# Causal attention in a two-layer hybrid model: queries and keys projected in the heads' own order, then moved to their fields

## The chip, the core and the metric

The kernel runs on one core of one Trainium2 chip. Its time is the device time of one execution in microseconds (us). A core has five engines with a queue of instructions each, which they work through in order: TensorE (PE; matrix products, with weight loads PEld listed apart), VectorE (DVE), ScalarE (ACT), GpSimd (POOL) and SyncE (SP, which issues DMAs). They wait for each other by semaphores. Matrix products read SBUF and write PSUM, which has eight banks of 128 partitions by 512 fp32 values.

## What is computed

A residual stream of 32 sequences of 256 tokens with 128 features passes through eight blocks. The change touches one of them, the last attention:

```python
x = x + _L1_attn_a_ref(_layernorm(x), ...)      # window attention with latents
x = x + _L1_ffn_ref(_layernorm(x), ...)         # 8 experts, 2 of them for each token
x = x + _L1_attn_b_ref(_layernorm(x), Wq, Wk, Wv, Wo)
x = x + _L1_ffn_ref(_layernorm(x), ...)

def _L1_attn_b_ref(x, Wq, Wk, Wv, Wo):          # 16 heads of 8 features
    Q, K, V = split(x @ Wq.T), split(x @ Wk.T), split(x @ Wv.T)
    Q, K = apply_rope(Q), apply_rope(K)         # turns pairs of neighbouring features
    scores = einsum(Q, K) / sqrt(8)             # causal, -inf for later keys
    out = softmax(scores) @ V
    return out @ Wo.T
```

## The kernel before

The stream is kept in SBUF, transposed, as 16 tiles `xs[c]` of 128 features by 512 tokens (a **chunk**: two sequences of 256). The stage `l1_attn_b` runs one generator, `chunk(c)`, for each of them; each `yield` ends a step. `pipeline(chunk, 16, newest=True)` (L336) starts a new chunk every 16 rounds and in each round takes one step of every active chunk, the newest first. A chunk has about 60 steps, so four chunks are in work at a time, 16 steps apart. What is written in this order is then put into queues by a scheduler, which may take a later instruction first where an earlier one is not ready; a tile waits for a free buffer of its tag.

The steps of a chunk, with their lines:

- Steps 0 to 8: `fetch` (L1420) reads the experts' rows of the block before and adds them to x (L1430 to L1434); `norm` (L323) centers (L326), squares, takes the mean (L311), the power -0.5 on GpSimd (L315) and spreads it (L320). L1634 gives `xin`, the normalised chunk.
- Steps 9 to 12, the part that changes: query and key are projected and turned. The 16 heads are laid out in two groups (y = 0, 1), 8 heads each with 16 partitions: 8 features and 8 spare ones, a **field**. The weights carry that layout already (`spaced`, L87), so that one 128x128 weight block makes one group. For each group and for q and k there are two products (L1643), one with the weights and one with the features of each pair swapped; VectorE multiplies them from PSUM with the cosine and the sine table (L1644); the two are added, for q by GpSimd (L1646), for k by VectorE (L1648), which also puts 1 into a spare feature of the field (the table `ninth`). `by_parity` (L940) then makes two masked copies of each key group on VectorE (L944).
- Steps 13 to 24: `attend` (L947) finds the largest score of each query: masks (L932), scores (L969, L996), reductions on VectorE (L978, L1000).
- Steps 25 to 28: the negated maximum is transposed (L1019) and added to the query's spare feature (L1021), masked copies `qb` (L944); the values are projected (L1149) and copied by VectorE (L1154).
- Steps 30 to 46: exponentials by key (L1038 and L1056 the scores, L1047 and L1060 the exponentials on ScalarE), GpSimd clears what is not causal (`keep_where`, L936), the weighted values (L1074), their copy on ScalarE (L1087), denominators (L1111) and their reciprocal `rden` (L1115), the result (L1119, L1120), the projection Wo (L1663).
- Steps 47 to 59: `send` (L1190) prepares the expert block: norm, router, shared expert, and eight indirect DMAs on GpSimd (L1301), which write the tokens into the experts' rows.

So the projections of a chunk (steps 9 to 12) stand in the same rounds as steps 25 to 28 of the chunk before, steps 41 to 44 of the one before that (L1074, L1087, L1111, L1115), and steps 57 to 58 of the third one before (L1301).

PSUM is handed out by tag: `st` has five banks for the scores, `av` one, and all else shares the tag `m` with two:

```python
ps = ph.enter_context(tc.tile_pool(name="cps", bufs=2, space=PSUM))
...
rps = ps.tile([P, CH], F32, tag="m", name="rps")
```

After the stage, `blocks1()` runs the experts on blocks of 256 rows (L1393, L1402); its first row loads wait for all of the rows that L1301 wrote.

Of the kernel before, what the change touches and what calls it, by code (L numbers as in the profile page):

```python
# [94 lines left out]
def pack_inputs(i):  # L95
    mam, com, att, row, taps = (Packed() for _ in range(5))
    turn = np.arange(DI).reshape(2, 32, 4).transpose(0, 2, 1).reshape(DI)

    p = "L0_attn_a_"
    for s in "fb":  # L100

        w = i[p + "in_w_" + s]
        mam.add("in_w" + s, np.concatenate([w[:DI], w[DI:][turn]]).T)


        xp = i[p + "xp_w_" + s]
        turned = [xp[at : at + DS].reshape(4, 4, DI).transpose(1, 0, 2).reshape(DS, DI) for at in (DTR, DTR + DS)]
        mam.add("xp" + s, halves(np.concatenate([xp[:DTR], *turned, np.zeros((1, DI), np.float32)]).T))
        mam.add("out" + s, i[p + "out_w_" + s][:, turn])
        dtp = np.zeros((DTR + 2 * DS + 1, DI), np.float32)  # L110
        dtp[:DTR], dtp[-1] = i[p + "dtp_w_" + s].T, i[p + "dtp_b_" + s]
        mam.add("dtp" + s, dtp)
        mam.add("conv_b" + s, i[p + "conv_b_" + s].reshape(1, -1))

        a = np.asarray(i[p + "A_log_" + s]).reshape(2, 32, 4, 4, 4)
        mam.add("A_log" + s, a.transpose(1, 4, 0, 3, 2).reshape(P, 32))
        mam.add("D" + s, halves(i[p + "D_" + s]))
        taps.add(s, i[p + "conv_w_" + s][:, 0, :].T.reshape(1, -1))
    mam.add("one_row", np.eye(DTR + 2 * DS + 1, dtype=np.float32)[:, -1:])
    mam.add("turn", np.eye(P, dtype=np.float32)[:, turn[:P]])  # L120
    mam.add("proj", halves(i[p + "proj_w"].T))
    mam.add("proj_b", col(i[p + "proj_b"]))
    mam.add("g", col(i[p + "ln_gamma"]))
    mam.add("minus", np.full((P, 1), -1.0))
    mam.add("b", col(i[p + "ln_beta"]))

    p = "L0_ffn_"
    com.add("pw", i[p + "pw_w"].T)
    com.add("dw", i[p + "dw_kernel"][:, 0, :])
    com.add("dw_b", col(i[p + "dw_bias"]))  # L130
    com.add("pw_b", col(i[p + "pw_b"]))
    com.add("rt0", i[p + "router_w"].T)
    com.add("exp_w", i[p + "expert_w"].transpose(2, 0, 1))
    com.add("exp_b", i[p + "expert_b"].T)
    com.add("f0_out", i[p + "out_w"].T)
    com.add("f0_out_b", col(i[p + "out_b"]))
    com.add("norm_w", col(i[p + "norm_w"]))
    com.add("ffd", i[p + "ff_down_w"].T)
    com.add("ffd_b", col(i[p + "ff_down_b"]))
    com.add("ffu", i[p + "ff_up_w"].T)  # L140
    com.add("ffu_b", col(i[p + "ff_up_b"]))
    row.add("rt0_b", i[p + "router_b"].reshape(1, -1))

    p = "L0_attn_b_"
    for n in "ABC":
        com.add("rnn" + n, i[p + n].T)
    com.add("rnn_g", col(i[p + "gamma"]))
    com.add("rnn_b", col(i[p + "beta"]))

    p = "L1_attn_a_"  # L150
    for n, part in (("q", 0), ("k", 1)):
        w = i[p + "qkv_w"][:, part * P : (part + 1) * P]
        b = i[p + "qkv_b"][part * P : (part + 1) * P].reshape(1, P)
        for x in range(2):
            att.add(f"a{n}{x}", spaced(w, x))
            att.add(f"ab{n}{x}", spaced(b, x).T)
    att.add("wv", i[p + "qkv_w"][:, 2 * P :])
    row.add("bv", i[p + "qkv_b"][2 * P :].reshape(1, -1))
    att.add("rq", i[p + "rq_w"])
    att.add("rq_b", col(i[p + "rq_b"]))  # L160
    att.add("rkv", i[p + "rkv_w"])
    att.add("rk_b", col(i[p + "rkv_b"][:32]))
    row.add("rv_b", i[p + "rkv_b"][32:].reshape(1, -1))
    att.add("rout", i[p + "rout_w"])
    att.add("rout_b", col(i[p + "rout_b"]))
    att.add("aout", i[p + "out_w"])
    att.add("aout_b", col(i[p + "out_b"]))
    for n in ("gl", "gr"):

        g = np.zeros((H, HD, H, HD), np.float32)  # L170
        for h in range(H):
            g[h, :, h, :] = i[p + n + "_w"]
        att.add(n, g.reshape(P, P))

    p = "L1_attn_b_"
    swap = np.arange(P) ^ 1
    for n in ("Wq", "Wk"):
        for x in range(2):
            att.add(f"{n}{x}", spaced(i[p + n].T, x))
            att.add(f"{n}s{x}", spaced(i[p + n][swap].T, x))  # L180
    att.add("Wv", i[p + "Wv"].T)
    att.add("Wo", i[p + "Wo"].T)

    p = "L1_ffn_"
    att.add("f1_g", col(i[p + "ln_gamma"]))
    att.add("f1_b", col(i[p + "ln_beta"]))
    att.add("rt1", i[p + "router_w"])
    att.add("sgu", i[p + "shared_gate_up_w"])
    att.add("sdn", i[p + "shared_down_w"])
    gu = np.ascontiguousarray(i[p + "gate_up_w"])  # L190
    dn = np.ascontiguousarray(i[p + "down_w"].reshape(E, FF // P, P, P).transpose(0, 2, 1, 3))

    return mam, com, att, row, taps, gu, dn


def shape_constants():
# [14 lines left out]
    for x in range(2):  # L211
        pk, dn = np.zeros((2, 8, 16, H, HD), np.float32)
        for h in range(8):
            pk[h, :HD, 8 * x + h, :] = np.eye(HD)
            dn[h, HD, 8 * x + h, :] = 1.0
        c1.add(f"pack{x}", pk.reshape(P, P))
        c1.add(f"den{x}", dn.reshape(P, P))
    c1.add("earlier", (np.arange(P)[:, None] < np.arange(P)[None]).astype(np.float32))
    c1.add("ones", np.ones((P, P), np.float32))
# [19 lines left out]
    inv = np.float32(10000.0) ** (-np.arange(half, dtype=np.float32) * np.float32(2.0) / np.float32(HD))  # L239
    ang = (np.arange(L, dtype=np.float32)[:, None] * inv[None]).astype(np.float32)  # L240
    at = (feat % HD) // 2
    used = (feat % 16 < HD)[:, None]
    cos = np.cos(ang)[:, at].T * used
    sin = np.sin(ang)[:, at].T * np.where(feat % 2 == 0, -1.0, 1.0)[:, None] * used
    c1.add("cosq", cos * SCALE)
    c1.add("sinq", sin * SCALE)
    c1.add("cosk", cos)
# [27 lines left out]
def hybrid_kernel(ctx: ExitStack, tc, x_d, out_d, d, packs):  # L275
# [1345 lines left out]
    def l1_attn_b(fetch, send):  # L1621
        with ExitStack() as ph:
            p1 = ph.enter_context(tc.tile_pool(name="c1", bufs=1))
            p2 = ph.enter_context(tc.tile_pool(name="c2", bufs=2))
            p3 = ph.enter_context(tc.tile_pool(name="c3", bufs=2))
            ps = ph.enter_context(tc.tile_pool(name="cps", bufs=2, space=PSUM))
            buffers = attention_buffers(p1)

            def chunk(c):
                x = xs[c]  # L1630
                yield from fetch(c, p2, ps, 4)
                xin = p2.tile([P, CH], F32, tag="xin", name="xin", bufs=2)
                xc, rb = yield from norm(p2, ps, x, 1)
                nc.vector.tensor_mul(xin, xc, rb)  # L1634
                yield
                rot, kb = {}, []
                for y in range(2):
                    for n in "qk":
                        t = p2.tile([P, CH], F32, tag=f"rot{n}{y}", name=f"rot{n}{y}", bufs=2 if n == "q" else 3)
                        u = p2.tile([P, CH], F32, tag="rot2", name="u")  # L1640
                        for w, tab, dst in ((f"W{n}{y}", "cos" + n, t), (f"W{n}s{y}", "sin" + n, u)):
                            rps = ps.tile([P, CH], F32, tag="m", name="rps")
                            nc.tensor.matmul(rps, W(w), xin, start=True, stop=True)  # L1643
                            nc.vector.tensor_mul(two(dst), two(rps), K(tab).unsqueeze(1).to_broadcast([P, 2, L]))  # L1644
                        if n == "q":
                            nc.gpsimd.tensor_add(t, t, u)  # L1646
                        else:
                            nc.vector.scalar_tensor_tensor(t, u, K("ninth"), t, ALU.add, ALU.add)  # L1648
                            kb.append(by_parity(p2, t, f"kb{y}", 1))
                        rot[n, y] = t  # L1650
                        yield
                o = p2.tile([P, CH], F32, tag="o", name="o")
                vbs, nms = buffers(c)

                def values(b):
                    project_values(ps, xin[:, b * L : (b + 1) * L], W("Wv"), None, vbs[b])
                    return vbs[b]

                yield from attend(
                    (p2, p3, ps), *([rot[n, y] for y in range(2)] for n in "qk"), kb, values, nms, masks_b, o  # L1660
                )
                ops = ps.tile([P, CH], F32, tag="m", name="ops")
                nc.tensor.matmul(ops, W("Wo"), o, start=True, stop=True)  # L1663
                nc.vector.tensor_add(x, x, ops)
                yield
                yield from send(c, p2, ps)

            pipeline(chunk, 16, newest=True)
# [47 lines left out]
```

## Time and profile before

| | us |
|---|---|
| median of 3 runs (6236.38 to 6243.42) | 6238.78 |
| the profiled execution | 6234.39 |
| its span, first to last instruction | 6232.7 |
| busy in the span: PE, PEld | 5356.8 (86%), 2792.6 (45%) |
| busy: DVE, ACT, POOL | 4117.2 (66%), 2710.2 (43%), 3289.4 (53%) |
| mean granted TensorE clock | 0.902 of full |

All numbers on lines and waits are of the profiled execution. A busy share is an average over stages with different limits: the recurrences of the first layer take the first half of the span, the window attention runs from about 3120 to 4150 us, the first expert pass to 4690, the stage of the change to about 5775, the second expert pass to the end.

The instructions that the change touches, over the whole stage: L1643 256 records (128 products of 128x512, each in two records), L1644 128 of 0.69 us, L1646 32 of 1.27 us, L1648 32 of 0.74 us at the median (1.04 in the mean), L944 on the keys 64 of 0.48 us.

In the answers of the trace a line gives the start and length in us, the engine, the line of the kernel, the operation with the tiles written and read, and in brackets the idle time of the engine before it with the instruction that ended it. Matrix products overlap, and their ends are modelled.

### The profile page before, as it was taken

How to read it: one execution, taken by the hardware profiler on the slowest of the kernel's cores; microseconds unless marked ns; L12 is line 12 of the kernel's file. 1: busy time of each engine (PE TensorE's matmuls, PEld its weight loads, DVE VectorE, ACT ScalarE, POOL GpSimd, SP SyncE). 2: the span in 40 equal slices, each digit the busy share in tenths (PEclk: the TensorE clock that was granted, in tenths of full speed). 3: DMA queues.
4: the chain of work that ended last, by engine and by line, in shares of the span. 5: the costliest groups of instructions: out<-in, count | busy, mean ns of one | idle time of the engine just before them, and what ended most of it. 6: DMA issues, size and time to landing. Idle time of an engine off the chain costs nothing. (4 is left out here: it accounts for less than half of the span.)

```text
span 6232.7 us, 73938 instructions
## 1 busy us (share of the span) xinstructions
PE 5356.8 (86%) x25850; PEld 2792.6 (45%) x25922; DVE 4117.2 (66%) x7006; ACT 2710.2 (43%) x4424; POOL 3289.4 (53%) x3074
## 2 busy tenths in 40 slices
PE   6777777777777799999998888897998999997997
PEld 2222222222221466965544444445884444443886
DVE  5998999989989554044555555655665666665565
ACT  4665666666655354344434444342221333333221
POOL 5888888888888564044634444443332333333332
PEclk9888988888988899598989999998998999998998
DMA  3333333333332740000000000004550000000555
GB/s 148 123 123 116 123 116 123 116 123 116 126 112 109 304 185 1 1 1 1 1 1 10 9 8 8 11 8 129 186 172 19 20 16 18 18 11 12 188 188 189
DMA packets 190421, 512.13 MB, mean 82 GB/s; under 512 B 22177, under 2 KB 75169, under 8 KB 164961
## 3 DMA queue, kind: packets, MB, share of 16 engines
q1 hardware_dynamic: 172192, 468.00, 21.1%
q0 software_dynamic: 17280, 35.69, 1.7%
q8 instruction: 205, 3.36, 0.2%
q10 hardware_dynamic: 576, 3.71, 0.2%
q14 instruction: 168, 1.37, 0.1%
HBM read 359.93 MB, written 147.38 MB: 81 GB/s over the span
## 5 line engine op out<-in xcount | busy, mean ns | idle before, releaser
L612 POOL TENSOR_TENSOR dBu<-widedu,bcB 128x512 f32<-128x512 f32 x1024 | 1294.8, 1284 | 249.9 <-DVE h L621 162.0
L621 DVE TENSOR_TENSOR_SCAN h<-dA,dBu 128x512 f32<-128x512 f32 x768 | 942.5, 1227 | 119.8 <-ACT dA L608 30.4
L574 PE MATMUL yps<-pr,cst_t 128*32 128x512 f32 x2048 | 579.9, 645 | 244.8 <-POOL pr L569 102.7
L936 POOL TENSOR_SCALAR_AFFINE_SELECT e<-e 128x2048 f32<-128x2048 f32 (+1 forms) x256 | 343.3, 1353 | 597.2 <-ACT e L1047 386.1
L1412 POOL DMA_INDIRECT rows_out<-y,goes x284 | 271.8, 957 | 559.9 <-DVE y L1410 464.2
L1000 DVE TENSOR_REDUCE nm<-st 128x2 f32<-128x512 f32 x512 | 324.3, 684 | 268.5 <-PE st L996 267.4
L608 ACT ACTIVATE dA<-widedelta,Af 128x510 f32<-128x510 f32 x512 | 348.5, 688 | 300.9 <-DVE h L621 222.0
L608 ACT ACTIVATE dA<-widedelta,Ab 128x510 f32<-128x510 f32 x512 | 345.0, 686 | 272.7 <-DVE h L621 209.5
L1187 ACT ACTIVATE s<-s 128x512 f32<-128x512 f32 x284 | 179.0, 630 | 578.3 <-DVE s L1186 309.2
L574 PEld LDWEIGHTS yps<-pr,cst_t 128*32 128x32 f32 x2048 | 86.8, 112 | 704.8 <-POOL pr L569 228.0
L315 POOL TENSOR_TENSOR rstd<-var,cst_t 128x4 f32<-128x4 f32 x128 | 130.0, 1016 | 516.2 <-DVE var L313 514.4
L781 POOL TENSOR_TENSOR comb<-comb,ye 128x512 f32<-128x512 f32 x224 | 284.8, 1275 | 182.0 <-DVE ye L780 75.2
L1060 ACT ACTIVATE e<-st 128x512 f32<-128x512 f32 x512 | 272.0, 598 | 184.5 <-PE st L1056 154.8
L569 POOL TENSOR_TENSOR pr<-hs,bcC 128x512 f32<-128x512 f32 x256 | 334.4, 1306 | 13.7 <-DVE hs L621 13.7
L621 DVE TENSOR_TENSOR_SCAN hs<-dA,dBu 128x512 f32<-128x512 f32 x256 | 308.3, 1204 | 48.8 <-ACT dA L608 47.3
L1301 POOL DMA_INDIRECT rows_in<-xt,slot x256 | 253.6, 991 | 119.0 <-issue 98.7
L623 DVE TENSOR_TENSOR pr<-h,bcC 128x1024 f32<-128x1024 f32 x256 | 309.8, 1210 | 8.5 <-PE yps L574 0.5
L1188 DVE TENSOR_TENSOR hh<-s,u_ps 128x512 f32<-128x512 f32 x284 | 195.4, 688 | 172.0 <-ACT s L1187 168.0
L1393 PE MATMUL g_ps<-xb,gu 128*128 128x256 f32 x1136 | 302.6, 389 | 3.6 <-ACT xb L1376 2.3
L1402 PE MATMUL yps<-dn,hh 128*128 128x128 f32 x2272 | 291.5, 276 | 5.9 <-DVE hh L1188 5.8
L1393 PE MATMUL u_ps<-xb,gu 128*128 128x256 f32 x1136 | 293.3, 381 | 0.0
L1402 PEld LDWEIGHTS yps<-dn,hh 128*128 128x128 f32 x2272 | 282.8, 192 | 15.3 <-DVE hh L1188 7.8
(353 smaller groups left out, 11248.5 us busy)
## 6 DMA issues: line engine op xcount, KB each, us to landing
gu<-in_gu SPq DMA_DIRECT2D x142, 512.0 KB, 3.7
rows_in<-zero SPq DMA_DIRECT2D x60, 1170.0 KB, 18.7
widedelta<-delta_d SPq DMA_DIRECT2D x64, 1024.0 KB, 5.5
widedu<-du_d SPq DMA_DIRECT2D x64, 1024.0 KB, 5.1
dn<-in_dn SPq DMA_DIRECT2D x142, 256.0 KB, 3.9
bcB<-xdbl_d SPq DMA_DIRECT2D x32, 1024.0 KB, 5.0
bcC<-xdbl_d SPq DMA_DIRECT2D x32, 1024.0 KB, 6.9
xr<-rows_in SPq DMA_DIRECT2D x142, 130.0 KB, 3.8
```

What stands on the lines that cost most here:

```text
L569: nc.gpsimd.tensor_mul(pr, hs, bc["C"][:, g, :])
L574: nc.tensor.matmul(yps[32 * k : 32 * k + 32, :], K("states"), pr, start=False, stop=(g == 3), skip_group_check=True, tile_position=(0, 32 ...
L608: nc.scalar.activation(two(dA)[:, :, 1:L], two(steps)[:, :, 1:L], AF.Exp, scale=A[s][:, at : at + 1])
L612: nc.gpsimd.tensor_mul(dBu, duw[:, k, :], bc["B"][:, g, :])
L621: scan[0] = nc.vector.tensor_tensor_scan(*views, 0.0, ALU.mult, ALU.add)
L623: nc.vector.tensor_mul(pr2, h2, bc["C"][:, g, :].unsqueeze(1).to_broadcast([P, 2, CH]))
L781: nc.gpsimd.tensor_add(comb, comb, ye)
L936: nc.gpsimd.affine_select(e, e, [[0, n], [sign, P]], ALU.is_gt, 0.0, base=base, channel_multiplier=-sign)
L1000: nc.vector.tensor_reduce(n1[:, x, 2 * r : 2 * r + 2], o.rearrange("p (j k) -> p j k", j=2), AX.X, ALU.max, negate=True,)
L1060: nc.scalar.activation(e0[:, r], o.rearrange("p (j k) -> p j k", j=2), AF.Exp)
L1393: nc.tensor.matmul(o[:, j, :], gu[:, at : at + P], xb, start=True, stop=True)
L1402: nc.tensor.matmul(yps[:, t, :], hh[:, k, t * P : (t + 1) * P], dn[:, k, :], start=(k == 0), stop=(k == FF // P - 1),)
```

## The change

The projections no longer carry the fields' layout. q and k are each made once, with all 16 heads in their own order, 128 partitions full; so two products each and not four. After the cosine and sine products GpSimd adds them, now for k too. A product with a 0/1 matrix `field{y}`, the transpose of `pack{y}`, puts eight of the heads into their fields, once for each group, in a PSUM tile of the tag `m`, and ScalarE copies it to `rot{n}{y}`; for k the copy adds the column `ninth` as its bias. The tables lose the zeros of the spare features. There are two more working tiles `t` (tag `rot1`, two buffers); the number of steps is the same.

```diff
-        for x in range(2):
-            att.add(f"{n}{x}", spaced(i[p + n].T, x))
-            att.add(f"{n}s{x}", spaced(i[p + n][swap].T, x))
+        att.add(n, i[p + n].T)
+        att.add(f"{n}s", i[p + n][swap].T)
...
         c1.add(f"pack{x}", pk.reshape(P, P))
+        c1.add(f"field{x}", pk.reshape(P, P).T)
...
-    used = (feat % 16 < HD)[:, None]
-    cos = np.cos(ang)[:, at].T * used
-    sin = np.sin(ang)[:, at].T * np.where(feat % 2 == 0, -1.0, 1.0)[:, None] * used
+    cos = np.cos(ang)[:, at].T
+    sin = np.sin(ang)[:, at].T * np.where(feat % 2 == 0, -1.0, 1.0)[:, None]
...
-                for y in range(2):
-                    for n in "qk":
-                        t = p2.tile([P, CH], F32, tag=f"rot{n}{y}", name=f"rot{n}{y}", bufs=2 if n == "q" else 3)
-                        u = p2.tile([P, CH], F32, tag="rot2", name="u")
-                        for w, tab, dst in ((f"W{n}{y}", "cos" + n, t), (f"W{n}s{y}", "sin" + n, u)):
-                            rps = ps.tile([P, CH], F32, tag="m", name="rps")
-                            nc.tensor.matmul(rps, W(w), xin, start=True, stop=True)
-                            nc.vector.tensor_mul(two(dst), two(rps), K(tab).unsqueeze(1).to_broadcast([P, 2, L]))
+                for n in "qk":
+
+                    t = p2.tile([P, CH], F32, tag="rot1", name="t")
+                    u = p2.tile([P, CH], F32, tag="rot2", name="u")
+                    for w, tab, dst in ((f"W{n}", "cos" + n, t), (f"W{n}s", "sin" + n, u)):
+                        rps = ps.tile([P, CH], F32, tag="m", name="rps")
+                        nc.tensor.matmul(rps, W(w), xin, start=True, stop=True)
+                        nc.vector.tensor_mul(two(dst), two(rps), K(tab).unsqueeze(1).to_broadcast([P, 2, L]))
+                    nc.gpsimd.tensor_add(t, t, u)
+                    yield
+                    for y in range(2):
+                        fps = ps.tile([P, CH], F32, tag="m", name="fps")
+                        nc.tensor.matmul(fps, K(f"field{y}"), t, start=True, stop=True)
+                        r = p2.tile([P, CH], F32, tag=f"rot{n}{y}", name=f"rot{n}{y}", bufs=2 if n == "q" else 3)
                         if n == "q":
-                            nc.gpsimd.tensor_add(t, t, u)
+                            nc.scalar.copy(r, fps)
                         else:
-                            nc.vector.scalar_tensor_tensor(t, u, K("ninth"), t, ALU.add, ALU.add)
-                            kb.append(by_parity(p2, t, f"kb{y}", 1))
-                        rot[n, y] = t
-                        yield
+                            nc.scalar.activation(r, fps, AF.Identity, bias=K("ninth"))
+                            kb.append(by_parity(p2, r, f"kb{y}", 1))
+                        rot[n, y] = r
+                    yield
```

## The prediction

> **What bounds the kernel now.** I read the page first (shares by engine, the chain that ended last), then the stage windows, then one chunk in the timeline. The chain that ended last lies in the second expert pass, after this stage, and takes over whatever this stage costs: the pass is gated by the last chunk's rows, so a delay here moves the end by as much. The chain's own head line, shares of the span:
>
> ```profile
> by line: PE g_ps L1393 2.0%; PE yps L1402 1.9%; PE u_ps L1393 1.8%; issue 0.4%; PE tps L1433 0.3%; PE xps L1374 0.2%; DMA xr<-rows_in 0.2%; DMA ys<-rows_out 0.1%; ACT s L1187 0.1%; DVE s L1186 0.0%; POOL rows_in L1301 0.0%; DVE ys L1430 0.0
> ```
>
> L1393 and L1402 are the experts' products. The attention stage itself is one long stretch of TensorE with short holes. Windows, columns: stretch, us, busy us (and instructions) of PE, PEld, DVE, ACT, POOL, granted clock, DMA share, GB/s:
>
> ```profile
> 4690.00:5775.00 1085.00, 983.13 (x5997) 481.24 (x6009) 684.82 (x1470) 336.51 (x576) 336.71 (x318) 0.89 0.05 16
> ...
> 5042.39:5103.67 61.28, 57.98 (x380) 28.89 (x377) 41.74 (x93) 20.97 (x36) 21.23 (x21) 0.95 0.06 18
> 5103.67:5171.19 67.52, 62.67 (x380) 30.72 (x377) 43.42 (x92) 21.03 (x36) 21.15 (x21) 0.88 0.05 17
> ...
> 5042.39:5061.70 19.31, 18.49 (x119) 8.26 (x115) 13.78 (x26) 2.65 (x5) 9.13 (x9) 0.99 0.07 23
> ```
>
> The stage takes 1085 us, a chunk (from one `xin` product to the next) 61.3 us at a clock of 0.95 and up to 67.5 us at 0.88: the same 380 matmul records, 6.2 us apart by the clock alone. The change lies in the chunk's first part, from `xin` to the first `rden`: 19.3 us, of which VectorE is busy 13.8 and ScalarE 2.65. TensorE's 18.5 there is modelled from pipelined ends; its issue tells more. Two weight loads of L1643 start 0.43 us apart, two records make one 128x512 product, so a product holds TensorE 0.86 us, and all products and transposes of this part come to some 14 us. Neither engine is full. A hand-over between PE, DVE and PE through the two `m` banks is what is slow, and the order of the queues decides. Timeline of a chunk (start, us, engine, line; in brackets the idle time before and who ended it):
>
> ```profile
> 5036.60 1.35 PE L932 MATMUL st<-mask_t 128*128 128x256 bf16 x3 [1.02 <-ACT e L1060]
> 5037.88 2.09 PE L996 MATMUL st<-kb,rotq 32*128 32x512 f32 x8
> ...
> 5042.39 0.68 DVE L1634 TENSOR_TENSOR xin<-xc,rb 128x512 f32<-128x512 f32 x1
> 5043.46 1.98 PE L1643 MATMUL rps<-xin,att_t 128*128 128x512 f32 x4
> 5045.55 0.69 DVE L1644 TENSOR_TENSOR u<-rps,cst_t 128x512 f32<-128x512 f32 x1 [0.24 <-PE rps L1643]
> 5045.95 1.51 PE L1074 MATMUL av<-e,vb 128*32 128x256 f32 x32
> 5047.39 1.98 PE L1643 MATMUL rps<-xin,att_t 128*128 128x512 f32 x4
> 5048.49 0.96 POOL L1301 DMA_INDIRECT rows_in<-xt,slot  x1 [0.30 <-issue]
> 5049.46 1.10 POOL L936 TENSOR_SCALAR_AFFINE_SELECT e<-e 128x1024 f32<-128x1024 f32 x1
> 5050.52 1.27 POOL L1646 TENSOR_TENSOR rotq<-rotq,u 128x512 f32<-128x512 f32 x1
> 5050.62 0.62 PE L1074 MATMUL av<-e,vb 128*32 128x256 f32 x2 [0.66 <-POOL e L936]
> ...
> 5061.76 3.39 DVE L1115 RECIPROCAL rden<-dps 128x128 f32<-128x128 f32 x4 [0.64 <-PE dps L1111]
> 5069.62 1.14 PE L996 MATMUL st<-kb,rotq 32*128 32x512 f32 x8
> ```
>
> Read POOL first. The query sum L1646 had its inputs at 5046.24 and ended at 5051.79: the eight indirect DMAs of the chunk three before and a select stand ahead of it. Now nobody needs that sum before the scores. I count t from 5042.39: products end by t = 3.0, `u` at 3.85, L1074 at 5.07, the sum at 9.40, `rden` begins at 19.37.
>
> **The change, by engine and chunk.**
> - TensorE: 8 products go, 4 products and 4 field products of the same shape come: 0.
> - VectorE: four L1644 (0.69) and two L1648 (0.74 at the median) go: -4.24 us, 68 us over 16 chunks. Nothing of this is on the clock by itself; it counts only if the hand-over shortens.
> - GpSimd: two sums of 1.27 us before (query halves), two after (query, key): 0.
> - ScalarE: two copies from PSUM (0.58, as L1219) and two Identity with a bias column, for which the other attention stage has the very form:
>
> ```profile
> L1571 ACT ACTIVATE qT<-pps,bq x32: 687/688/712, 3130.2 to 4102.6; 128x512 f32<-128x512 f32 x32
> ```
>
> Together 2.5 us, in a part where ScalarE works 2.65 of 19.3 us and waits for the `av` copy. Hidden; without that cover the `m` bank would be late by up to one exponential group, 2.06 us.
> A rule speaks against this move: the Trainium skill, "ScalarE: Activation LUTs", section "Rules for kernel authors", gives adds and multiplies to VectorE. By it the four evictions would stay there at 0.69 each, 2.8 us; the rows give ScalarE 0.58 to 0.69 for the same size out of PSUM. I go by the rows.
> - Weights and constants: `att` loses 512 columns, `cst1` gains 256; both are in place before 3119 us, where the other attention stage first reads `att`; this stage begins at 4690: 0. The extra `t` buffers cost nothing.
>
> **The added wait.** The first field product reads the sum, so it cannot start before t = 9.40. What is ready on TensorE ends at 5.07. Behind the waiting product stand, in `m` order, the transposes of the second half (L1019), both key products, the values and the denominators. The `m` tiles stand on TensorE in program order in every chunk I read, with two banks; so I take it that none of them passes the field products. Only the other half of L1074 may, and it waits for the select until 8.2. Hence a hole of 3.1 to 4.3 us. Now forward at full clock. An eviction starts 1.16 us after its product does (5043.46 to 5044.62).
> - Field q0, q1: 9.4 to 11.1; copies end at 11.2 and 12.05.
> - Key products wait for those banks: 12.1 to 13.8; the second multiply ends at about 14.8.
> - Key sum on POOL, now free: 14.9 to 16.2.
> - Field k0, k1: 16.2 to 17.9; Identity ends 18.1 and 18.9; the two `kb` pairs (0.87 each) end at 19.9, where the last `kb` now ends at 18.7.
> - The last values and L1111 wait on the same banks: `rden` at about 21.4 instead of 19.4.
>
> The lower bound of this wait: POOL takes the sum as soon as `u` is there, as in the chunk at 4788.60, which has no DMAs ahead (sum done at t = 4.9). Then all is 4.5 us earlier: `rden` at 16.9. The upper bound is set by the clock.
>
> **The clock.** L996 x8 takes 1.14 us at 5069.62 and 2.09 at 5037.88, right after some 3 us in which TensorE had only small work; the same happens in each chunk that I opened. It then lasts 5.6 us (full again at 5043.46) or, in the 64 to 67 us chunks, 11 us, to about t = 6.5. A hole of 4 us should do the same. The skill's "TensorE: Matmul & The Clock Gate", Part 1, wants a window of 3.4 us at rest, and the window runs free: a 4.3 us hole holds a whole one in about (4.3 - 3.4)/3.4 = 26% of the cases (my estimate). By the row a lightly used stretch is enough nearly always. With half clock from 9.4 to about 15, the field products, transposes and key products (4 x 0.86 + 0.6) take 4 us longer, of which I put 2.9 on the path: `rden` at 24.3. I go by the row, 9 chunks in 10; by the page's chance it would be 21.4 + 0.26 x 2.9 = 22.2.
>
> **The sum.** `xin` to `rden` of chunks 3 to 15 as they are: seven at 19.3 to 20.3 (mean 19.6), six at 22.3 to 24.0 (mean 22.9), together 274 us. In the six long ones the late start is hidden behind the same POOL time, so all thirteen come to one value. With the row: 13 x 24.0 = 312, +38. By the page's chance: 13 x 22.2 = 289, +15. Chunks 1 and 2 without DMAs: -1.4 each; chunk 0 has a longer bare chain: +4. Together +1. Forecast: about +38 us. The profiled execution (span 6232.7, time 6234.39) becomes 6273, and with the median of the runs, 4.4 us above it, 6277. I say 6276.
>
> **Rivals.**
> 1. The clock holds: 13 x 21.4 = 278, +4, and +1: 6244, no measurable change. For it: the hole is only just longer than a gate window; against it: the dip of each chunk.
> 2. Faster: the sum is not late. If GpSimd's order puts it ahead of the DMAs, or other work fills the hole, the seven short chunks gain 2.7 us and the six long ones 2.8: 7 x 2.7 + 6 x 2.8 = 35 us, 6204. It decides when the sum ends before about t = 7. For it: 4.2 us of VectorE gone from the part and the chunk at 4788.60. Against it: DMAs stood ahead of the sum in each later chunk opened, though they come later in the program.
> 3. Slower than forecast: the clock stays at half to the end of the part, as in the 67.5 us chunks. Then the six products on the path are all at double length: 21.4 + 6 x 0.86 = 26.5 us each, 345 in all, +71: 6310. For it: six of thirteen chunks already carry a dip this far; against it: none carries it to `rden`.
>
> **Chances and range.** Forecast 0.50, rival 3 0.14, rival 1 0.16, rival 2 0.20. Measurement tells 0.2% (12.5 us) from no change. Slower 0.64, same 0.16, faster 0.20. Range 6210 to 6312: it reaches down to most of rival 2 and up to rival 3; for the forecast alone 6258 to 6295.
>
> **What will show it.** In the profile after: field products with idle time before them ended by POOL's sum, 3 us or more in chunks 3 to 15 and near zero in chunks 1 and 2; `xin` to `rden` at 21 to 25 us; key products at about double length after the hole; VectorE's busy time down by some 68 us and ScalarE's up by some 40; the expert passes as before. I am wrong if the key products stand ahead of the query's field products on TensorE, if POOL's sum precedes the DMAs, or if the clock row of the stage stays at 0.89 or rises.

## The result, and the profile after

Before: 6243.42 us median (6236.38 to 6251.60, 5 runs). After: 6279.95 us median (6270.02 to 6304.39, 5 runs). The ratio is 1.0059 (95% interval 1.0036 to 1.0082): slower by 36.5 us. The profiled execution of after is the longest of its five, 6304.39 us with a span of 6302.7, so its sums run to 70 us where the medians say 37. Below the diff the lines of after stand one earlier than before (L1301 is L1300, L1074 is L1073, L936 is L935); the new ones are L1642 (projections), L1643 (multiplies), L1644 (sum), L1648 (field products), L1651 and L1653 (ScalarE's copies).

The chain that ended last still lies in the second expert pass:

```profile
by line: PE g_ps L1392 1.8%; PE yps L1401 1.7%; PE u_ps L1392 1.5%; DMA xr<-rows_in 0.7%; issue 0.3%; PE tps L1432 0.2%; DMA ys<-rows_out 0.2%; PE xps L1373 0.2%; ACT s L1186 0.1%; DVE s L1185 0.1%; DVE hh L1187 0.1%; DVE ys L1429 0.1%; POO
```

The window of one chunk of after from `xin` to `rden`, in the same columns (from this `xin` to the next, at 5088.39, the chunk takes 68.4 us):

```profile
5019.98:5044.70 24.72, 19.96 (x107) 8.57 (x104) 9.21 (x21) 4.91 (x9) 9.17 (x9) 0.86 0.05 18
```

It answers to the 19.31 us at a clock of 0.99 before. VectorE has lost 4.6 us there, ScalarE has gained 2.3, and the part is 5.4 us longer, at 0.86. The timeline of this chunk shows where:

```profile
5019.98 0.67 DVE L1633 TENSOR_TENSOR xin<-xc,rb 128x512 f32<-128x512 f32 x1
5020.71 1.98 PE L1642 MATMUL rps<-xin,att_t 128*128 128x512 f32 x4
5023.27 1.51 PE L1073 MATMUL av<-e,vb 128*32 128x256 f32 x32
5026.12 0.96 POOL L1300 DMA_INDIRECT rows_in<-xt,slot  x1 [0.30 <-issue]
5027.09 1.10 POOL L935 TENSOR_SCALAR_AFFINE_SELECT e<-e 128x1024 f32<-128x1024 f32 x1
5028.15 1.26 POOL L1644 TENSOR_TENSOR t<-t,u 128x512 f32<-128x512 f32 x1
5029.47 3.78 PE L1648 MATMUL fps<-t,cst_t 128*128 128x512 f32 x4 [4.69 <-POOL t L1644]
5031.59 0.58 ACT L1651 COPY rotq<-fps 128x512 f32<-128x512 f32 x1 [9.83 <-PE fps L1648]
5035.03 2.16 PE L1642 MATMUL rps<-xin,att_t 128*128 128x512 f32 x4
5038.00 1.27 POOL L1644 TENSOR_TENSOR t<-t,u 128x512 f32<-128x512 f32 x1 [8.58 <-DVE u L1643]
5039.66 1.98 PE L1648 MATMUL fps<-t,cst_t 128*128 128x512 f32 x4
5044.70 3.39 DVE L1114 RECIPROCAL rden<-dps 128x128 f32<-128x128 f32 x4 [1.09 <-PE dps L1110]
```

Read the first L1648: 4.69 us idle, ended by GpSimd's sum, and then 3.78 us for the four records that take 1.98 ten microseconds later. That is a hole and then half the clock. The sum itself ran 1.26 us; it came late because the indirect DMAs and a select stood ahead of it. The group of this line shows that it is so in the whole stage:

```profile
L1648 PE MATMUL fps<-t,cst_t 128*128 128x512 f32 x128 | 80.3, 760 | 57.2 <-POOL t L1644 57.1
```

The last columns are TensorE's idle time just before the group and who ended it: 57 of 57 us by one engine and one line.

Adding up the profiled executions: the stage begins 19.9 us later (nothing that runs ahead of it was changed, and two traces of the kernel before differ by 11.7 us there), the first three chunks take 8.1 us more, chunks 3 to 14 together 37.4 more, and from the last `xin` to the end 4.6 more. That is 70.0. Of the 37.4, 28.3 lie between `xin` and `rden` and 9.1 between `rden` and the next `xin`.

### The profile page after: what moved, and what is told of

The parts are those of the page before. It is cut to its first block, busy times and chain, and to the rows that moved or that the text cites. A ratio compares the mean times of both kernels' runs of the same rounds, so it can differ in the third digit from the quotient of the medians.

```text
span 6302.7 us, 74006 instructions
## 1 busy us (share of the span) xinstructions
PE 5390.4 (86%) x25922; PEld 2793.8 (44%) x25922; DVE 4050.2 (64%) x6910; ACT 2747.8 (44%) x4488; POOL 3287.0 (52%) x3074
## 3 DMA queue, kind: packets, MB, share of 16 engines
q10 hardware_dynamic: 576, 3.71, 0.1%
## 5 line engine op out<-in xcount | busy, mean ns | idle before, releaser
L935 POOL TENSOR_SCALAR_AFFINE_SELECT e<-e 128x2048 f32<-128x2048 f32 (+1 forms) x256 | 343.0, 1352 | 614.9 <-ACT e L1046 404.6
L1300 POOL DMA_INDIRECT rows_in<-xt,slot x256 | 253.8, 992 | 119.0 <-issue 98.5
```

The source lines that it names most:

```text
L935: nc.gpsimd.affine_select(e, e, [[0, n], [sign, P]], ALU.is_gt, 0.0, base=base, channel_multiplier=-sign)
```

## The experiments

Three sets of runs on three chips, each with the kernel before beside it. "A" is the mean of `xin` to `rden` over chunks 3 to 15 of the profiled execution; "clock" is the granted clock over these parts, weighted by their lengths. The single value of after's ratio is given above; the intervals of the table are of each run against the kernel before beside it.

| run | us, median | before beside it | ratio, 95% interval | A, us | clock in A |
|---|---|---|---|---|---|
| before | | | | 21.08 | 0.93 |
| after | 6279.95 | 6243.42 | 1.0036 to 1.0082 | 23.42 | 0.88 |
| e1_sum_dve | 6274.36 | 6238.40 | 1.0051 to 1.0076 | 22.12 | 0.88 |
| e2_half_dmas | 6210.65 | 6238.40 | 0.9948 to 0.9972 | 19.11 | 0.90 |
| e3_fill | 6259.34 | 6238.40 | 1.0024 to 1.0051 | 22.61 | 0.92 |
| e4_keys_first | 6240.54 | 6238.40 | 0.9992 to 1.0008 | 20.24 | 0.92 |
| a0_again | 6289.49 | 6275.08 | 1.0008 to 1.0034 | 23.26 | 0.88 |
| e6_dmas_behind | 6226.50 | 6275.08 | 0.9907 to 0.9933 | 18.70 | 0.93 |
| e7_keys_first_behind | 6261.52 | 6275.08 | 0.9966 to 0.9986 | 20.42 | 0.97 |
| b1_before_behind | 6224.42 | 6275.08 | 0.9909 to 0.9938 | 19.16 | 0.95 |
| b0_before_again | 6242.34 | 6239.48 | 0.9992 to 1.0011 | 21.07 | 0.93 |
| e6_again | 6213.58 | 6239.48 | 0.9941 to 0.9971 | 19.12 | 0.90 |
| e8_two_fills | 6205.47 | 6239.48 | 0.9934 to 0.9962 | 17.29 | 1.00 |
| e9_one_fill | 6189.64 | 6239.48 | 0.9902 to 0.9930 | 17.29 | 1.00 |

**The sum taken off GpSimd.**

```diff
-                    nc.gpsimd.tensor_add(t, t, u)
+                    nc.vector.tensor_add(t, t, u)
```

> The two sums of a chunk go from GpSimd to VectorE, all else as changed. Hole theory: the field products no longer wait for the sum, but in this build the first L1073 of the other half stands ahead of them on TensorE and needs GpSimd's select, which still comes after the eight DMAs, at t = 8.2 (t from the start of the xin product). So the hole stays at about 3 us and is ended by L935 in place of the sum; the field products start at about t = 8.4 and not 9.5, and the key sum costs 0.8 us and not 1.4. xin to rden: some 20 us at full clock, 23 with a dip, against 21.7 and 24.7 of the changed kernel; the kernel 6245 to 6262 us. Rival, the cost is the longer chain through PSUM and ScalarE: VectorE gets 1.5 us more work in each chunk, nothing is won, 6275 to 6290.

A miss: 6274 us, 36 above before and next to the band of the rival (6275 to 6290). The time alone cannot tell the two apart; the trace can. Timeline of one chunk of this run:

```profile
5050.86 0.68 DVE L1644 TENSOR_TENSOR t<-t,u 128x512 f32<-128x512 f32 x1
...
5053.72 1.11 POOL L935 TENSOR_SCALAR_AFFINE_SELECT e<-e 128x1024 f32<-128x1024 f32 x1
5054.89 1.06 PE L1073 MATMUL av<-e,vb 128*32 128x256 f32 x2 [3.25 <-POOL e L935]
5055.88 3.78 PE L1648 MATMUL fps<-t,cst_t 128*128 128x512 f32 x4
```

The sum is ready at 5051.54, but the next thing on TensorE, the weighted values of an older chunk, waits for the select that stands behind the same DMAs. In this chunk the hole shrinks from 4.69 to 3.25 us and the half clock follows all the same. That is so in four of the thirteen chunks (holes of 3.25 to 4.52 us), where after has eight; in the other nine TensorE waits for the select 2.05 us at most, and the field products run at full clock. So the sum is only one of two things that stand behind the DMAs and hold TensorE up.

**Half of the DMAs away.** Of each token's two rows only the first is written, in the last expert block only; the other is left out of the output.

```diff
-                for k in range(2):
+                for k in range(1 + (n_ffn == 0)):
```

> Leaves out one of the two rows that each token sends to the last expert block (four indirect DMAs of a chunk and not eight), so that block reads rows that were not written. Hole theory: GpSimd is 5 us earlier at the sum, which then ends at t = 4.5 to 5.5, the hole before the query's field products is under 1 us in every chunk, no half clock follows it, and xin to rden is 17 to 18.5 us in chunks 3 to 15: some 75 us less than the changed kernel, 6195 to 6215. Rival, the longer chain and ScalarE: the DMAs do not touch it, xin to rden stays above 21 us and the kernel within 10 us of the changed one.

The time is as expected, 69 us under after. From the third chunk on the longest wait of a field product is 0.28 us:

```profile
5300.01 1.98 PE L1648 MATMUL fps<-t,cst_t 128*128 128x512 f32 x4 [0.27 <-POOL t L1644]
```

The chunk through PSUM, ScalarE and back is not too long by itself: at full clock it takes 17.29 us, less than any chunk of before from the third on. A is 19.11 and not 17 to 18.5, because ten of the thirteen chunks start at half clock. Rows left out may save time elsewhere too, so this run alone does not price the hole; the DMAs moved, further down, do.

**The hole filled.** Four products that nobody reads, after the query sum is issued.

```diff
                     nc.gpsimd.tensor_add(t, t, u)
+                    if n == "q":
+                        fill = ps.tile([P, CH], F32, tag="st", name="fill", bufs=5)
+                        for _ in range(4):
+                            nc.tensor.matmul(fill, W("Wq"), xin, start=True, stop=True)
                     yield
```

> Puts four products of 128x512 whose result nobody reads behind the query's two projections, in a free bank of the scores, so that TensorE works 3.4 us of the hole. Clock theory: the hole that is left is about 1.5 us, the half clock after it goes, and xin to rden is 21.7 us in all of chunks 3 to 15, as now in four of thirteen: 9 x 2.7, some 25 us less, 6250 to 6262 us, in spite of 55 us more work of TensorE. Rival, the dips have nothing to do with the hole: nothing is won or up to 15 us lost, 6278 to 6295.

The time is as expected, 6259 us. From the third chunk on all field products run 1.98 us, none 3.78; in four chunks they still wait for the sum, up to 1.8 us after the filling. Work for nothing gains 20 us, and the clock in A rises from 0.88 to 0.92. A itself falls less than expected, to 22.61 and not 21.7, since in most chunks the filling starts late, behind a start at half clock. How the loss divides between the clock and the hole this run does not show.

**The keys first.** Both sums before the first field product, so that the key projections fill the hole.

```diff
+                turned = {}
                 for n in "qk":
...
                     nc.gpsimd.tensor_add(t, t, u)
+                    turned[n] = t
                     yield
+                for n in "qk":
                     for y in range(2):
                         fps = ps.tile([P, CH], F32, tag="m", name="fps")
-                        nc.tensor.matmul(fps, K(f"field{y}"), t, start=True, stop=True)
+                        nc.tensor.matmul(fps, K(f"field{y}"), turned[n], start=True, stop=True)
```

> The same instructions in another order: the key's projections, products and sum come in the second of the four steps, the query's field products in the third, the key's in the fourth. Hole theory: TensorE does the key's projections and the second transposes while the sum waits behind the DMAs; the field products still start at t = 9.4, but the hole before them is 1 to 2 us, and the key's chain is done 4 us earlier: xin to rden 17 to 18.5 us, and the kernel 6200 to 6215 us, below the kernel before (6238). Rival, the added transfer through PSUM, ScalarE and a second product is itself too long: the order wins at most 10 us, 6265 to 6280.

It takes back the loss, 6240.5, and no more: 25 us short of what was expected. A is 20.24, not 17 to 18.5. Its timeline:

```profile
5056.80 3.48 DVE L943 TENSOR_SCALAR qb<-qn,cst_t 128x512 f32<-128x512 f32 x2
5057.26 1.11 POOL L935 TENSOR_SCALAR_AFFINE_SELECT e<-e 128x1024 f32<-128x1024 f32 x1
5058.32 1.27 POOL L1644 TENSOR_TENSOR t<-t,u 128x512 f32<-128x512 f32 x1
...
5060.94 0.66 PE L1018 MATMUL nt<-cst_t,nm 128*128 128x128 f32 x4 [1.71 <-DVE t L1643]
```

VectorE's two masked copies take 3.48 us, 0.88 in the chunk of after shown above, and end 0.7 us after GpSimd's select and sum beside them; TensorE waits for the multiplies behind. And seven of the thirteen chunks have a clock of 0.82 to 0.92 in A, most of them from their start, as in before.

**The DMAs moved.** GpSimd is idle for 13.5 us after the key sum of after, and the eight DMAs take 10.1. In the next runs they stand there; nothing is left out. The changed kernel with this move is called the moved kernel below. (In `b1_before_behind` the anchor is the second query sum of before, and the diff is otherwise the same.)

```diff
+    sums = []
...
+            for _ in range(4 * n_ffn):
+                yield
             for t in range(4):
-                for k in range(2):
-                    i = nc.gpsimd.indirect_dma_start(
+                with tc.issue_after(sums[-1].ins) if n_ffn and sums else nullcontext():
+                    for k in range(2):
+                        i = nc.gpsimd.indirect_dma_start(
...
-                    nc.gpsimd.tensor_add(t, t, u)
+                    i = nc.gpsimd.tensor_add(t, t, u)
+                    if n == "k":
+                        sums.append(i)
```

> The changed kernel once more, nothing edited, as the yardstick on the same chip for the three others. Expected 6265 to 6290 us. If the slowdown found first belongs to one chip or one moment, it comes out within 6230 to 6250. In its trace the field products should wait 2.1 to 5.6 us for GpSimd's sum in each chunk from the third on, as in the first trace of it.

> The changed kernel with the 8 indirect DMAs of the older chunk put behind the sums of the newest chunk in GpSimd's queue (the trace of the changed kernel shows GpSimd idle for 13.5 us there, and the 8 take 10.1); nothing is left out. The theory of the hole (TensorE waits for a sum that stands behind these DMAs, then runs at half clock) expects the stretch from xin to rden at 17.3 to 19.5 us where the changed kernel had 23.4 on average, no field product waiting over 0.5 us, and 6195 to 6215 us. The rival that the chain through PSUM and ScalarE itself is too long expects no gain: 6265 us or more. The rival that the DMAs only hold something else up at their new place (the select of the next attend step) expects 6225 to 6260.

> As the last, and with all four projections and both sums ahead of the field products (the order of the earlier run with the keys first, which came out equal to the kernel before). If that run's remaining loss was GpSimd's late sum and select standing beside VectorE's query copies and a TensorE left idle, both go with the DMAs: xin to rden 17 to 18.5 us, 6185 to 6205 us. If the half clock at the start of its chunks came from the stretch before xin, it stays: xin to rden 20 to 21, 6225 to 6245.

> The kernel before with the same move of the 8 DMAs behind its second query sum: the fair comparison, since the move might help any kernel. If the DMAs cost time only because the change makes TensorE wait for the sum behind them, the kernel before gains little: 6225 to 6245. If they already held its attention up through the select that stands behind them, it gains as much as the changed one: 6195 to 6215, and then the change has no part of its own in the gain.

After itself took 6289 us, as expected, and its field products wait 56.7 us for the sum, as in the first trace. But the kernel before took 6275 on this chip, 37 more than on the first. The sign of the difference holds (1.0008 to 1.0034); its size does not carry over from chip to chip. No trace of before was taken here, so why it is slower on this chip stays open.

The move gains 63 us against after, as the theory of the hole had it, though the time is 6226, 11 us above the expected band. It lies in the band of the rival that the DMAs hold something else up at their new place. The trace speaks against that one: from `rden` to the next `xin` chunks 3 to 14 take 512 us, and 514 in after on this chip. What is left in A is the half clock at the start of seven of the thirteen chunks. Timeline:

```profile
5009.43 1.51 PE L1073 MATMUL av<-e,vb 128*32 128x256 f32 x32
5011.21 1.98 PE L1655 MATMUL fps<-t,cst_t 128*128 128x512 f32 x4 [0.27 <-POOL t L1649]
...
5018.60 1.98 PE L1655 MATMUL fps<-t,cst_t 128*128 128x512 f32 x4
```

L1655 is the field product here. It waits 0.27 us where it waited 4.69, and the key's does not wait.

With the keys first as well it is slower, 6261.5, and neither expectation fits. VectorE's masked copies are down to 1.40 us, so that part of the reading of the earlier run was right; and only 4 of 13 chunks start at half clock (clock 0.97 in A). Yet A is 20.42, and 18.8 to 20.3 where the clock is full. Another wait has come: the copy of the weighted values on ScalarE, in front of the key's own copies, is released by the key's field products here,

```profile
4998.51 0.59 ACT L1086 COPY avs<-av 128x512 f32<-128x512 f32 x1 [4.14 <-PE fps L1657]
```

and by the weighted values themselves with the queries first (in the run with one fill, below):

```profile
5059.22 0.59 ACT L1086 COPY avs<-av 128x512 f32<-128x512 f32 x1 [4.91 <-PE av L1073]
```

So the order of the original change is the better one once the DMAs are out of its way. That this wait is the reason, no run tests.

The run on before was the one that changed the picture. It gains 51 us and comes out equal to the moved kernel (6224.4 and 6226.5, six runs each that spread over 26 and 16 us). The time stands just under the band for "gains little", but the bands were set for a kernel before of 6238 us, and it has 6275 here: a gain of 51 us is more than either allowed. So the DMAs already held up the kernel before. Two groups of TensorE in before and in this run, in which the last columns are again idle time and its releaser:

```profile
L1074 PE MATMUL av<-e,vb 128*32 128x128 f32 (+1 forms) x2048 | 111.1, 340 | 11.8 <-POOL e L936 11.8
L1019 PE MATMUL nt<-cst_t,nm 128*128 128x128 f32 x128 | 22.1, 299 | 9.3 <-DVE rotk L1644 9.3
```

```profile
L1074 PE MATMUL av<-e,vb 128*32 128x128 f32 (+1 forms) x2048 | 110.5, 339 | 6.2 <-POOL e L936 6.2
L1019 PE MATMUL nt<-cst_t,nm 128*128 128x128 f32 x128 | 21.2, 289 | 0.0
```

The first wait, for the select itself, shrinks by 5.6 us. The second, for VectorE, shrinks by 9.3 and is gone. It stood in the six long chunks of before, where VectorE's masked copies of the query stand beside GpSimd's select and sum and take 3.0 to 3.7 us; with the DMAs moved they take 1.4 to 1.5 in every chunk. One pair in before and one in this run:

```profile
5177.78 3.34 DVE L944 TENSOR_SCALAR qb<-qn,cst_t 128x512 f32<-128x512 f32 x2
```

```profile
5167.72 1.41 DVE L944 TENSOR_SCALAR qb<-qn,cst_t 128x512 f32<-128x512 f32 x2
```

A falls by 1.92 us on average, 25 us over thirteen chunks. The two waits make about 15 us of it, and the clock, which rises from 0.929 to 0.953, about 8 (274 us at the one lose 19.4, 249 at the other 11.8). The trace of before is of another set of runs than this one; its second trace, in the last set, has the same A. From the first `xin` to the last this run takes 889 us, where the two traces of before have 918 and 917. So the traces show 28 to 29 of the 51 us; the rest goes with the slower time of before on this chip, and stays open.

**What the half clock before `xin` costs.** In the moved kernel many chunks still take 19.4 to 20.6 us from `xin` to `rden`, the others 17.3 to 17.7: seven of thirteen in its first trace, ten in its second. The last set adds to it one or two products that nobody reads, just ahead of the mask matmuls that wait for ScalarE, 4 to 6 us before `xin` (two here; `e9_one_fill` has one):

```diff
-                xc, rb = yield from norm(p2, ps, x, 1)
+                g = norm(p2, ps, x, 1)
+                for k in range(2):
+                    next(g)
+                    yield
+                fill = ps.tile([P, CH], F32, tag="st", name="fill", bufs=5)
+                for _ in range(2):
+                    nc.tensor.matmul(fill, W("Wq"), x, start=True, stop=True)
+                xc, rb = yield from g
```

> The kernel before, nothing edited, for a second trace of it. The times of the kernel before were 6238 us in one set of runs and 6275 in another, while the changed kernel had 6280 and 6289; so the size of the difference is not settled. If the kernel before has its own waits for GpSimd's select behind the DMAs, and they decide chunk by chunk whether TensorE falls to half clock, then its stretch from xin to rden should spread from 19 to 24 us again, with another share of long ones; the ratio against itself is 1.000.

> The changed kernel with the DMAs behind the sums, again, as the yardstick for the next two. Expected 0.990 to 0.996 of the kernel before, 6215 to 6235 us; in its trace 8 of 14 chunks start at half clock (xin to rden 19.4 to 20.6 us) and 6 at full (17.3 to 17.7).

> The same, with 2 matmuls per chunk added that nobody reads (a weight matrix by x, into a PSUM tile of its own), in TensorE's queue just ahead of the mask matmuls that wait 1.0 and 0.2 us each for ScalarE, 4 to 6 us before xin. If the half clock at the start of these chunks comes from that thinly used stretch, it goes: xin to rden 17.3 to 17.7 in all chunks, 15 to 20 us less than the yardstick, 6200 to 6215 us. If the clock does not hang on this stretch, the added 2 us per chunk only cost: 6235 to 6260 us.

> As the last with 1 added matmul instead of 2, about 1 us. If the stretch decides, but 2 us of filling stand in the way of the masks, this one is the better: 6205 to 6220 us. If the filling does nothing for the clock: equal to the yardstick or up to 15 us above.

Before repeats itself (A 21.07; 6 of its 13 chunks long, 22.3 to 23.9). The moved kernel goes chunk by chunk as the run with half of the DMAs left out did, within 0.1 us of its `xin` to `rden` in each, and has the same ratio (0.9960 there, 0.9956 here). So what that run gained was most likely the hole, and not the rows it did not write; the two were taken on different chips. With the fills every chunk of both runs takes 17.29 or 17.30 us at a clock of 1.00. The same place in the moved kernel and in the one with one fill:

```profile
5041.17 0.28 PE L931 MATMUL st<-mask_t 128*128 128x256 bf16 x1
5042.47 0.27 PE L931 MATMUL st<-mask_t 128*128 128x256 bf16 x1 [1.02 <-ACT e L1059]
5042.96 0.86 PE L931 MATMUL st<-mask_t 128*128 128x256 bf16 x2 [0.22 <-ACT e L1059]
5043.75 2.09 PE L995 MATMUL st<-kb,rotq 32*128 32x512 f32 x8
```

```profile
5040.32 1.10 PE L1643 MATMUL fill<-x,att_t 128*128 128x512 f32 x2
5041.62 0.27 PE L931 MATMUL st<-mask_t 128*128 128x256 bf16 x1 [0.19 <-ACT e L1059]
5042.11 0.27 PE L931 MATMUL st<-mask_t 128*128 128x256 bf16 x1 [0.22 <-ACT e L1059]
5042.60 0.27 PE L931 MATMUL st<-mask_t 128*128 128x256 bf16 x1 [0.22 <-ACT e L1059]
5043.09 0.27 PE L931 MATMUL st<-mask_t 128*128 128x256 bf16 x1 [0.22 <-ACT e L1059]
5043.29 1.14 PE L995 MATMUL st<-kb,rotq 32*128 32x512 f32 x8
```

The same eight scores (L995) take 2.09 us in the one and 1.14 in the other. The 1.10 us of filling lies where TensorE waited 1.02, so it costs nothing: from `rden` to the next `xin`, summed over chunks 3 to 14, the run with one fill takes 506.0 us and the moved kernel 505.7. (That wait is for exponentials, ahead of which ScalarE loads a table for 1.28 us, at 5040.53 in the moved kernel. No run does without the load.) One fill gives 6189.6 us, 24 under the moved kernel beside it, more than expected, and the fastest of all. Two give 6205.5, as expected: the chunks gain the same 24 us in A, but the way from `rden` to the next `xin` is 527 us; what takes longer there stays open. Over the stage from the first `xin` to the last, the windows of after, the moved kernel and the one with one fill:

```profile
4718.78:5682.53 963.75, 868.30 (x5270) 413.40 (x5271) 542.81 (x1185) 324.95 (x554) 283.08 (x266) 0.89 0.05 15
```

```profile
4710.87:5598.15 887.28, 840.90 (x5270) 402.78 (x5271) 537.96 (x1186) 325.06 (x554) 283.69 (x263) 0.92 0.05 16
```

```profile
4713.89:5579.08 865.19, 823.00 (x5302) 395.03 (x5301) 538.65 (x1185) 325.94 (x556) 283.61 (x263) 0.98 0.05 16
```

In before this stretch took 918.2 us at 0.91. The fill was not tried on the kernel before with the DMAs moved, so these runs do not show whether the change has a part of its own in the 6189.6 us.

## Why the prediction was right, and where it was not

Direction and mechanism held: the sum behind the DMAs, the hole, the half clock after it. The size, 6276 forecast and 6280 measured, is in part luck: the terms of the sum missed by -8, +7 and +9 us and in part cancel, and on the second chip the same change cost 14 us and not 37. By its steps:

- **Busy times.** VectorE -68 forecast, -67.0 measured (4117.2 to 4050.2); ScalarE +40, +37.6; GpSimd 0, -2.4. ScalarE's copies take 0.585 and 0.687 us, as the rows that were taken for them. None of this set the time, as said.
- **The hole.** Forecast 3.1 to 4.3 us, the lower end if the second half of the weighted values filled part of it; measured 4.69 in the chunk shown. That half stands behind the field products on TensorE there (5034.04), so nothing filled it. Moving the DMAs away closed it, so the DMAs as its cause are shown.
- **The clock.** "A hole of 4 us should do the same": yes, the field products after such a hole took 3.78 us. The row of the trace, and not the chance of one in four worked out from the page, was the right one to go by.
- **`rden` at 21.4 and 24.3.** Measured 21.71 and 23.9 to 25.0. The lower bound of 16.9 came close: chunks at full clock in which nothing waits take 17.29.
- **The step that failed is "all thirteen come to one value", with a dip in 9 of 10 chunks.** Eight of thirteen had it (mean 24.5); five, whose start was already at half clock, had not. There the query projections themselves run slow and end later, so the hole is shorter, and the field products run at full clock. One such chunk of after:

```profile
5158.14 3.74 PE L1642 MATMUL rps<-xin,att_t 128*128 128x512 f32 x4
...
5165.89 1.98 PE L1648 MATMUL fps<-t,cst_t 128*128 128x512 f32 x4 [2.13 <-POOL t L1644]
```

  The late start was hidden behind GpSimd's time, as forecast, but it also saved the second dip. So the thirteen come to 304 us and not 312: +30, where +38 was put down.
- **Chunks 0 to 2.** Forecast together +1. Chunk 2 gained 1.0, but the first three took 8.1 more: in chunk 0 both sums made TensorE wait 2.1 us each.
- **From `rden` to the next `xin`** nothing was forecast; it grew by 9 us. The 8 us too much on the thirteen chunks and the 16 too little here and in chunks 0 to 2 are more than noise: in the second trace of after the thirteen come to 302 us, chunks 0 to 2 to 159 (153 and 151 in the two traces of before, 161 in the first of after), and this way to 514 (511 twice, and 520).
- **"6.2 us apart by the clock alone"** is a misreading. The granted clocks, 0.95 of 61.28 us and 0.88 of 67.52, make about 5 us of it. In the long chunk TensorE also waits 2.01 us (at 5114.25) for VectorE, whose masked copies take 3.71 us there.
- **"Now nobody needs that sum before the scores"** is true of the sum and misled me on the queue. A line of my own timeline had L1074 waiting 0.66 us for the select behind the same DMAs. I read it as nothing; moving those DMAs in the kernel before was worth 51 us on the one chip where it was tried, 28 to 29 of them seen in the traces.
- **Rival 2** set the point at a sum done before t = 7, and 6204 us. With the DMAs moved the sum ends in time, and the two sets gave 6226 and 6214. As the change stood it was not to be had.
- **A mark that was badly chosen:** "wrong if the clock row of the stage stays at 0.89". Over a window of 1085 us from the start of the stage it is 0.89 in both kernels, since the part that changes is a quarter of it. Over the parts from `xin` to `rden` it fell from 0.93 to 0.88.

The 67 us of VectorE that the change saves have bought nothing so far: with the DMAs out of the way both kernels take the same time within 2 us. At full clock the part from `xin` to `rden` is shorter by 1.0 us in the changed kernel (17.29 and 18.29), but more of its chunks start at half clock. What a chunk of this stage takes is set by who waits for GpSimd's queue and by TensorE's clock.

## What to carry to other kernels

When a result moves onto a new path, look at what stands ahead of its producer in that engine's queue, not at the producer's own time; here a sum of 1.3 us cost 37 us on one chip and 14 on another, because ten microseconds of DMA issue stood before it in each chunk. A wait of a few tenths of a microsecond that such a queue already causes is a reason to try another order of the queue on the old kernel as well; look also at what its late work runs beside. And where TensorE is thinly used for some 3 us in front of a busy part, one product that nobody reads, put exactly where it would wait, can be worth more than the wait: here 1.1 us of work per chunk brought 24 us, on one chip.

## What the runs showed of the hardware

- TensorE fell to half clock without a long pause: the longest idle time in the stretch before L995 was 1.02 us, with small matmuls before and after it. The Trainium skill, "TensorE: Matmul & The Clock Gate", Part 1, speaks of a window of some 3.4 us at rest; here a sparse one was enough, and a single product of 1.10 us in it was enough to prevent it, in 13 of 13 chunks. How sparse it has to be, these runs do not show.
- In chunks 3 to 15 of the two traces of after all sixteen holes of 4.3 to 5.6 us were followed by half clock, and the ten of 1.1 to 2.6 us were not.
- An indirect DMA holds GpSimd's queue for 0.96 us and 0.30 more until the next one, eight of them 10.1 us, though their transfers take next to none of the DMA engines (a share of 0.05 in the windows).
- VectorE's pair of masked copies (L943) took 3.48 us instead of 0.88 while GpSimd ran a select and a sum, and 1.40 when it ran only a sum. The Trainium skill, "GPSIMD Engine Reference", section "Key points", has the two engines share their interfaces to SBUF, with contention for some forms of VectorE's instructions; the times fit it, but no run here shows that these copies are of such a form.
